# Two weight sums on GpSimd, a gate of one matmul, the first patches in one queue, and other tiles for the last image

## The chip, the cores and the metric

The kernel runs on one core of a Trainium2 chip. The metric is the device time of one execution in microseconds. Before the change the median of three runs is 2782.4 us (2776.88 to 2785.29). The profile is a further execution, with its own time.

## What is computed

The input is x, 16 images of 256 channels, 28x28, float32. The layer adds to x a block applied to its group norm:

```python
v = gn(x)                                            # 32 groups
h = relu(bn1(amm_conv3x3(v, centroids1, wsub1)))
h = bn2(amm_conv3x3(h, centroids2, wsub2))
s = sigmoid(relu(mean_hw(h) @ w1 + b1) @ w2 + b2)    # 256 -> 16 -> 256
out = x + relu(h * s[:, :, None, None] + v)
```

`amm_conv3x3` takes, for each channel and pixel, the nine values of the 3x3 patch, a softmax over 16 centroids by negative squared distance, the mean of the centroids under it (nine values again), and a product of these 256 x 9 values with `wsub`, a 2304 x 256 matrix.

## The kernel before

The work is a list of jobs. `at(cluster, sub, f, ...)` puts each under a key, and at the end (L1038) the keys are sorted and the jobs written out, so the order of each engine's instructions is the order of the keys. A layer of one image is eight clusters (`g = 8 * n`), for four blocks of (half of the channels, half of the pixels); each block takes two clusters of input, and its later steps lie in the clusters of the blocks behind it.

A block's steps: `patches` (L337) copies the shifted rows of the padded image ("home" in DRAM) into one of two tiles `pt`, in six transfers: three of 16 partitions by 8 (L342, always on SP's queue) and three of 8 by 8 (L346, on SP's queue, or on GpSimd's where `single` says so). `logits` (L351) are 32 small matmuls (64 records) in each cluster, `exps` (L365) their exponentials on ScalarE into tiles `e` of a pool with six buffers. `num_b` (L411) and `num_a` (L398) are the sums under the exponentials. VectorE inverts the denominators (L443) and spreads them over partitions (L458); the quotients q, tiles `qp` and `qo`, are made on GpSimd (L466) or VectorE (L477).

The product with wsub, a matrix of two by two parts, is done with seven products instead of eight. `mix` (L490) subtracts quotients of two blocks on GpSimd (five instructions for a pair of blocks: one at L492, four at L494). `combine` (L183) makes the summed weights S1, S2, S3, S4 of the first layer on VectorE; S2 = S1 - A11 and S4 = A12 - S2. `product` (L481) is nine matmuls into a PSUM bank, and `acc_copy` and `acc_add` (L515, L519) bring banks into the regions of the output; the eight banks are one ring. `PRODUCTS` says which weights a cluster's product reads: cluster 8 S3, 9 S2, 10 S4.

For the gate `se_hidden` (L751) multiplies the channel sums with w1 (four matmuls; w1, w2 and b1 padded to 128 columns or rows) and `se_gate` (L766) the hidden vector with w2 (two matmuls, one for each half of the channels). The weights are loaded by `load_se` (L202) in cluster 92, one of the tiles being that of `nhalf`. The images but the last have their closing passes spread over later clusters (`finish_gate`, `finish_norm`, `finish_sum`, `finish_relu`, `finish_add`); the last image uses `finish_norm` and `finish_fast` (L786, L805). `finish_norm` writes the group norm of x into the tile `xn` of tag "pb", of which there is one buffer. `flags` (L823), which checks the range of the denominators, uses the same tag for its tile `ok`.

Of the kernel before, what the change touches and what calls it, by code (L numbers as in the profile page):

```python
# [8 lines left out]
F32 = mybir.dt.float32  # L9
I32 = mybir.dt.int32  # L10
U32 = mybir.dt.uint32
AF = mybir.ActivationFunctionType
ALU = mybir.AluOpType
# [4 lines left out]
P = 128  # L18
# [5 lines left out]
N = RT * W  # L24
# [12 lines left out]
NPT = 2  # L37
# [30 lines left out]
def kernel(  # L68
# [20 lines left out]
    nc = tc.nc  # L89
    B, C, _ = x.shape  # L90
    NB = C // P
    RED = se_w1.shape[1]

    const = ctx.enter_context(tc.tile_pool(name="const", bufs=1))
    dram = ctx.enter_context(tc.tile_pool(name="dram", bufs=1, space=DRAM))
    small = ctx.enter_context(tc.tile_pool(name="small", bufs=2))
# [6 lines left out]
    def bank(name):  # L103
        return p_ring.tile([P, 512], F32, tag="ps", name=name)
# [21 lines left out]
    io = ctx.enter_context(tc.tile_pool(name="io", bufs=1))  # L126
    wpool = ctx.enter_context(tc.tile_pool(name="wpool", bufs=1))
    epool = ctx.enter_context(tc.tile_pool(name="epool", bufs=6))
# [54 lines left out]
    def combine(n):  # L183
        a, b, op = {
            "S1": ("S3", "A22", ALU.add), "S2": ("S1", "A11", ALU.subtract),
            "S4": ("A12", "S2", ALU.subtract), "S3": ("A11", "S3", ALU.subtract),
        }[n]
        nc.vector.tensor_tensor(wl[n], wl[a], wl[b], op)

    nhalf_sb = load(nhalf, "nhalf_sb")  # L190
    load_wd(None, 0)
# [3 lines left out]
    load_wd(None, 1)  # L195
    load_cw(0, 1)
    vecs = load(vec, "vecs", nc.gpsimd)
    w1_sb = [nhalf_sb, const.tile([P, P], F32, name="w1_sb")]
    w2_sb = const.tile([P, C], F32, name="w2_sb")
    b1_sb = const.tile([P, 1], F32, name="b1_sb")  # L200

    def load_se():  # L202
        for t in (*w1_sb, w2_sb, b1_sb):
            nc.gpsimd.memset(t, 0.0)
        for k in range(NB):
            nc.sync.dma_start(w1_sb[k][:, :RED], se_w1[k * P : (k + 1) * P, :])
        nc.sync.dma_start(w2_sb[:RED], se_w2)
        nc.sync.dma_start(b1_sb[:RED], se_b1.rearrange("(p o) -> p o", o=1))


    m_lo, m_hi, zero = kst[:, 0:1], kst[:, 1:2], kst[:, 2:3]
    m_cw = kst[:, 3:7]
# [283 lines left out]
    ys = {}  # L496
# [252 lines left out]
    se = {}  # L749

    def se_hidden(b):  # L751
        ysum = ys[b, "sum"]
        ps = bank("sep")[:, :1]
        n = 0
        for k in range(NB):
            for i in range(2):
                nc.tensor.matmul(
                    ps, lhsT=w1_sb[k], rhs=ysum[:, k, i : i + 1],
                    start=(n == 0), stop=(n == 2 * NB - 1),
                )  # L760
                n += 1
        hid = small.tile([P, 1], F32, name="se_hid")
        nc.scalar.activation(hid, ps, AF.Relu, bias=b1_sb, scale=1.0 / HW)
        se[b] = hid

    def se_gate(b):  # L766
        hid = se[b]
        ps = bank("sep")[:, :NB]
        for k in range(NB):
            nc.tensor.matmul(  # L770
                ps[:, k : k + 1], lhsT=w2_sb[:, k * P : (k + 1) * P], rhs=hid, start=True, stop=True
            )
        gt = small.tile([P, NB], F32, name="se_gt")
        for k in range(NB):
            nc.scalar.activation(
                gt[:, k : k + 1], ps[:, k : k + 1], AF.Exp, bias=nb2_sb[:, k : k + 1], scale=-1.0
            )
        nc.vector.tensor_scalar_add(gt, gt, 1.0)  # L778
        nc.vector.reciprocal(gt, gt)  # L779
        se[b] = gt  # L780
# [4 lines left out]

    def finish_norm(b, k):  # L786
        if k == 0:
            ys[b, "t"] = io.tile([P, 1568], F32, tag="pb", name="xn")
        nc.scalar.activation(
            ys[b, "t"][:, HW * k : HW * k + HW], xs[b][:, k], AF.Identity,  # L790
            bias=nrm[:, b, 2, k : k + 1], scale=nrm[:, b, 1, k : k + 1],
        )
# [28 lines left out]
    fi = const.tile([1, 1], I32, name="fi")  # L821

    def flags():  # L823
        ok = io.tile([P, 1568], F32, tag="pb", name="ok")[:, : 16 * B].rearrange("p (a n) -> p a n", a=2)
        nc.vector.tensor_scalar(ok[:, 0], wsum, LIM, None, op0=ALU.is_le)
        nc.vector.tensor_scalar(ok[:, 1], wsum, 0.0, None, op0=ALU.is_ge)
        nc.vector.tensor_reduce(fl[:, 0:1], ok.rearrange("p a n -> p (a n)"), axis=AX.X, op=ALU.min)
        nc.vector.tensor_scalar(fl[:, 0:1], fl[:, 0:1], -1.0, 1.0, op0=ALU.mult, op1=ALU.add)
        nc.vector.tensor_reduce(fl[:, 2:3], csum, axis=AX.X, op=ALU.max)
        nc.vector.tensor_scalar(fl[:, 2:3], fl[:, 2:3], CLIM, None, op0=ALU.is_gt)  # L830
        nc.vector.tensor_add(fl[:, 0:1], fl[:, 0:1], fl[:, 2:3])
        nc.vector.memset(fl[:, 3:4], 1.0)
# [8 lines left out]
    def at(cl, sub, f, *a, **kw):  # L841
        jobs.setdefault((cl, sub), []).append((f, a, kw))
# [20 lines left out]
    for j, u in enumerate(blocks):  # L863
        g = 2 * j
        u["w"] = j
        wide = u["l"] == 1 and u["hh"] == 0
        for p in range(2):
            u["pt", p] = pts[p]
            at(g + p - NPT, 0.5, patches, u, p, nc.gpsimd if g + p < 5 else None)
            for q in range(2):  # L870
                mm = 2 * p + q
                at(g + p, 0.1 + 0.1 * q, logits, u, mm)
                if wide and mm == 0:
                    at(g, 0.12, wide_copy, u, mm)
                    at(g, 0.9, wide_turn, u, mm)
                    at(g, 0.95, wide_sub, u, mm)
                    at(g + 1, 0.3, wide_back, u, mm)
                    at(g + 1, 0.9, wide_exp, u, mm)
                else:
                    at(g + p, 0.12 + 0.1 * q, exps, u, mm)  # L880
        at(g + 2, 1.3, num_b, u)
        at(g + 2, 1.4, split_b, u)
        at(g + 2, 1.5, join_b, u)
        at(g + 2, 1.6, recip_dve, u)
        at(g + 2, 1.7, spread, u, 4)
        at(g + 2, 1.71, scale_q, u, 4)
        for mm in range(2):
            at(g + 2, 1.35, num_a, u, mm)
            at(g + 2, 1.45, copy_a, u, mm)
            at(g + 3, 1.8, spread, u, mm)  # L890
            at(g + 3, 1.8, scale_q, u, mm)
        for mm in range(2, 4):
            at(*((g + 2, 1.8) if mm == 2 else (g + 3, 0.05)), spread, u, mm)
            at(g + 3, 1.0, num_a, u, mm)
            at(g + 3, 1.1, scale_a, u, mm)

    for l in range(2):
        for b in range(B):
# [26 lines left out]
            if l == 0:  # L925
                for o in range(2):
                    if b == 0:
                        at(g + 12 + o, 0.35, rank_score, o)
                        at(g + 12 + o, 0.6, rank_keep, o)
                        at(g + 12 + 2 * o, 0.65, h0_keep, o)  # L930
                    else:
                        for r in range(2):
                            at(g + 12 + o + (o and r), (0.5, 2.9)[r] if o == 0 else (2.4, 2.9)[r], to_home2, b, o, r)
                if b + 1 < B:
                    at(*((g - 1, 2.6) if b else (2, 1.65)), load_x, b + 1)
                    for q in range(NB):
                        at(g + (1 + q if b else 4), 0.3, gn_stats, b + 1, q)
                    at(g + (3 if b else 4), 2.1, gn_mean, b + 1)
                    at(g + 4, 2.1 if b else 2.2, gn_var, b + 1)
                    for q in range(NB):  # L940
                        at(g + 5, 0.9 if b else 0.3, gn_apply, b + 1, q)
                        at(g + 5, 1.9 if b or q else 0.9, to_home1, b + 1, q)
            else:
                last = b == B - 1
                at(*((g + 11, 0.6) if last else (g + 13, 2.6)), load_x, b, last)
                at(g + 13, 2.1, se_hidden, b)
                at(g + 14, 1.05 if last else 2.1, se_gate, b)
                for q in range(NB):
                    at(g + (13 if last else 19), 0.9, finish_norm, b, q)
                    if not last:  # L950
                        at(g + 19, 0.91, finish_gate, b, q)
                        at(g + 20, 0.05, finish_sum, b, q)
                        at(g + 20, 0.9, finish_relu, b, q)
                        at(g + 21, 0.05, finish_add, b, q)
                        at(g + 21, 0.06, store, b, q)
                    else:
                        at(g + 14, 1.92, finish_fast, b, q)
                        at(g + 14, 1.92, store, b, q)
                if b == B - 1:
                    at(g + 11, 0.95, flags)  # L960
                    at(g + 12, 2.9, flag_sum)

    at(1, 1.65, load_w, 0, "A11")
    at(3, 1.65, load_w, 0, "S3")
    at(3, 1.65, load_w, 0, "A22")
    at(6, 0.6, load_w, 0, "A12")
    for c, m in ((5, "S1"), (7, "S2"), (8, "S4"), (6, "S3")):
        at(c, 1.96, combine, m)
    for hh in range(2):
        at(6, 2.7, keep_wd, hh)  # L970
    for o in range(2):
# [223 lines left out]
```

## Time and profile before

| | |
|---|---|
| median of the runs | 2782.4 us |
| profiled execution | 2758.4 us |
| its span | 2756.9 us |
| instructions | 88069 |
| mean granted TensorE clock | 0.988 |
| MATMUL L485, w_S and w_A with qp | 708.3 and 521.2 us busy |
| MATMUL L356 (logits) | 535.2 us busy |
| MATMUL L403 and L417 | 409.0 and 371.2 us busy |
| POOL L494 (mixes) | 938.6 us busy, 1863 ns each |

In the profile, a row of a group says: line, engine, operation, what it writes and reads with shapes, count, busy time. PE is TensorE's matmuls, PEld its weight loads, DVE VectorE, ACT ScalarE, POOL GpSimd, SP the engine that issues most transfers. In a timeline each row has its start and length in us from the start of the span, and in brackets the idle time of the engine ahead of it with what ended it. float32 matmuls appear as two records each. The last 17.8 us of the span lie behind the last product on PE, and the first 28.9 before the first logits.

### The profile page before, as it was taken

The page shows a single profiled execution, that of the slowest core. Times are in us where ns is not written, and L with a number is a line of the kernel's source. Part 1 is how long each engine was busy: PE and PEld are TensorE (multiplying, and loading weights), DVE is VectorE, ACT ScalarE, POOL GpSimd, SP SyncE. Part 2 cuts the span into 40 slices and gives each one's busy share as a digit, 9 for nine tenths or more (in the row PEclk, how much of TensorE's full clock was granted, in tenths as well). Part 3 has the DMA queues.
Part 4 walks back from the last instruction along what each step waited for, and adds up shares of the span by engine and source line. Part 5 has one row for each costly group of instructions (what it writes and reads, how often), then busy time and mean ns, then how long its engine had stood idle before and what let it go on. Part 6 is the DMA issues. An engine that isn't in the chain of part 4 may idle for free. (4 is left out here: it accounts for less than half of the span.)

```text
span 2756.9 us, 88069 instructions
## 1 busy us (share of the span) xinstructions
PE 2670.6 (97%) x37076; PEld 1312.1 (48%) x37076; DVE 1730.1 (63%) x3945; ACT 1454.2 (53%) x3277; POOL 2073.0 (75%) x1427
## 2 busy tenths in 40 slices
PE   5699999999999999999999999999999999999997
PEld 2344444444444444444444455444444444444444
DVE  4866555565655565655576766666766666766664
ACT  3344455545455445455445566656565656555653
POOL 4656877668877767866678787788887788877787
PEclk9899999999999999999999999999999999999998
DMA  8564677546677656666575455445455545555541
GB/s 194 135 131 115 181 196 198 154 110 158 158 189 188 155 125 156 161 165 152 120 182 121 102 120 123 116 103 114 114 120 122 116 105 111 116 118 122 117 106 47
DMA packets 223281, 374.51 MB, mean 136 GB/s; under 512 B 30424, under 2 KB 193592, under 8 KB 222880
## 3 DMA queue, kind: packets, MB, share of 16 engines
q1 hardware_dynamic: 215744, 334.53, 52.6%
q0 software_dynamic: 7136, 34.27, 3.6%
q8 instruction: 296, 4.85, 0.8%
q14 instruction: 105, 0.86, 0.1%
HBM read 288.91 MB, written 79.80 MB: 134 GB/s over the span
## 5 line engine op out<-in xcount | busy, mean ns | idle before, releaser
L368 ACT ACTIVATE e<-lg 128x392 f32<-128x392 f32 x1920 | 777.7, 527 | 814.6 <-PE lg L356 812.3
L494 POOL TENSOR_TENSOR qp<-qp,qp 128x784 f32<-128x784 f32 x512 | 938.6, 1863 | 22.9 <-DVE qp L477 22.9
L485 PE MATMUL acc<-qp,w_S 128*128 128x392 f32 x2048 | 708.3, 496 | 5.2 <-POOL qp L494 5.2
L466 POOL TENSOR_TENSOR qp<-qp,rb 128x784 f32<-128x784 f32 x256 | 470.7, 1861 | 204.4 <-DVE rb L458 204.4
L356 PE MATMUL lg<-pt,wd 32*32 32x392 f32 x16384 | 535.2, 503 | 43.9 <-DVE half_sum L522 18.7
L458 DVE STREAM_SHUFFLE rb<-r 128x392 f32<-128x392 f32 x1024 | 551.2, 603 | 0.0
L485 PEld LDWEIGHTS acc<-qp,w_S 128*128 128x128 f32 x2048 | 387.4, 191 | 306.0 <-issue 15.9
L485 PE MATMUL acc<-qp,w_A 128*128 128x392 f32 x1536 | 521.2, 492 | 0.0
L437 DVE SCALAR_TENSOR_TENSOR r<-nb,kst,r 128x392 f32<-128x392 f32 x128 | 79.8, 623 | 563.4 <-ACT r L428 547.3
L403 PE MATMUL na<-e,cwa 64*32 64x392 f32 x8192 | 409.0, 496 | 3.9 <-issue 3.9
L485 PEld LDWEIGHTS acc<-qp,w_A 128*128 128x128 f32 x1536 | 291.8, 190 | 213.8
L417 PE MATMUL nb<-e,cwb 64*32 64x392 f32 x8192 | 371.2, 496 | 0.0
L356 PEld LDWEIGHTS lg<-pt,wd 32*32 32x32 f32 x16384 | 232.0, 103 | 274.8 <-issue 171.4
L443 DVE RECIPROCAL r<-r 128x392 f32<-128x392 f32 x128 | 331.8, 2592 | 0.0
L466 POOL TENSOR_TENSOR qo<-qo,rb 128x392 f32<-128x392 f32 x128 | 131.1, 1024 | 259.2 <-DVE rb L454 259.1
L477 DVE TENSOR_TENSOR qp<-na,rb 128x392 f32<-128x392 f32 x512 | 252.3, 555 | 64.6 <-PE na L403 61.7
L403 PEld LDWEIGHTS na<-e,cwa 64*32 64x32 f32 x8192 | 146.4, 106 | 230.2 <-ACT e L368 125.0
L417 PEld LDWEIGHTS nb<-e,cwb 64*32 64x32 f32 x8192 | 143.2, 107 | 220.6 <-issue 138.3
L471 ACT COPY qp<-na 128x392 f32<-128x392 f32 x512 | 211.6, 513 | 3.9 <-PE na L403 3.9
L428 ACT ACTIVATE r<-nb,kst 128x392 f32<-128x392 f32 x128 | 87.6, 685 | 102.7 <-PE nb L417 100.1
L492 POOL TENSOR_TENSOR qo<-qo,qo 128x392 f32<-128x392 f32 x128 | 130.8, 1022 | 2.2
L374 ACT COPY e<-lg 128x392 f32<-128x392 f32 x128 | 52.9, 500 | 150.6 <-PE lg L356 150.6
(146 smaller groups left out, 1810.7 us busy)
## 6 DMA issues: line engine op xcount, KB each, us to landing
pt<-home SPq DMA_DIRECT2D x768, 209.0 KB
pt<-home SPq DMA_DIRECT2D x753, 104.5 KB
home<-xpad SPq DMA_DIRECT2D x31, 899.0 KB
xt<-in_x SPq DMA_DIRECT2D x30, 784.0 KB
out_dram<-y SPq DMA_DIRECT2D x32, 392.0 KB
w_S<-d_wS SPq DMA_DIRECT2D x4, 576.0 KB
st<-in_wsub SPq DMA_DIRECT2D x4, 512.0 KB
st<-d_wa SPq DMA_DIRECT2D x16, 128.0 KB
```

Of the source, the lines that this page charges most:

```text
L356: nc.tensor.matmul(bk[32 * c : 32 * c + 32, :N].rearrange("p (r w) -> p r w", w=W), lhsT=wts["wd", u["hh"]][32 * i : 32 * i + 32, mm, c, : ...
L368: nc.scalar.activation(eg[:, i, :], bk[:, :N], AF.Exp, scale=2.0)
L403: nc.tensor.matmul(bs[r][32 * i : 32 * i + 32, :N], lhsT=wts["cwa", u["hh"]][64 * r : 64 * r + 64, mm, i, :], rhs=es[64 * r : 64 * r + 64, ...
L417: nc.tensor.matmul(bs[r][32 * i : 32 * i + 32, :N], lhsT=wts["cwb", u["hh"]][64 * r : 64 * r + 64, mm, i, :], rhs=es[64 * r : 64 * r + 64, ...
L443: nc.vector.reciprocal(u["r"], u["r"])
L458: nc.vector.stream_shuffle(rb[:, r, :], u["r"], mask_of(2 * mm + r))
L466: nc.gpsimd.tensor_tensor(q, q, u.pop(("rb", mm)), ALU.mult)
L471: nc.scalar.copy(u["q", 2 * mm + r], bk[:, :N])
L477: nc.vector.tensor_mul(u["q", 2 * mm + r], bk[:, :N], rb[:, r, :])
L485: nc.tensor.matmul(accs[key][:, :N], lhsT=wl[w][:, k, :], rhs=us["q", k], start=first and n == 0, stop=last and n == len(ks) - 1,)
L492: nc.gpsimd.tensor_tensor(out_u["q", 8], in0["q", 8], in1["q", 8], ALU.subtract)
L494: nc.gpsimd.tensor_tensor(pair(out_u, mm), pair(in0, mm), pair(in1, mm), ALU.subtract)
```

## The change

`combine` issues S2 and S4 on GpSimd; S2's key goes from sub 1.96 to 2.65 of cluster 7, behind that cluster's mixes. The first patches (the key of g + p = 0) have all six transfers on SP's queue. w1 is stored twice side by side, 32 columns, so that the hidden vector lies twice in 32 partitions; a constant `halves` with ones in the upper 16 rows of column 0 and the lower 16 of column 1 multiplies it on ScalarE, and one matmul with both halves of w2 stacked in 32 rows gives both columns of the gate. `load_se` clears nothing and makes six transfers instead of four. In the last image `xn` and `ok` are tiles `e`; `finish_norm` goes from (g + 13, 0.9) to (g + 12, 0.4), ahead of the relus of the image before it in ScalarE's order, and `flags` from sub 0.95 to 0.65 of cluster g + 11.

```diff
-        nc.vector.tensor_tensor(wl[n], wl[a], wl[b], op)
+        (nc.gpsimd if n in ("S2", "S4") else nc.vector).tensor_tensor(wl[n], wl[a], wl[b], op)
...
-    w1_sb = [nhalf_sb, const.tile([P, P], F32, name="w1_sb")]
-    w2_sb = const.tile([P, C], F32, name="w2_sb")
-    b1_sb = const.tile([P, 1], F32, name="b1_sb")
+    w1_sb = const.tile([P, NB, 2 * RED], F32, name="w1_sb")
+    w2_sb = const.tile([2 * RED, P], F32, name="w2_sb")
+    b1_sb = const.tile([2 * RED, 1], F32, name="b1_sb")
+    halves = const.tile([2 * RED, NB], F32, name="halves")
+    nc.gpsimd.memset(halves, 0.0)
+    nc.gpsimd.memset(halves[:RED, 0:1], 1.0)
+    nc.gpsimd.tensor_scalar(halves[:, 1:2], halves[:, 0:1], -1.0, 1.0, op0=ALU.mult, op1=ALU.add)
 
     def load_se():
-        for t in (*w1_sb, w2_sb, b1_sb):
-            nc.gpsimd.memset(t, 0.0)
         for k in range(NB):
-            nc.sync.dma_start(w1_sb[k][:, :RED], se_w1[k * P : (k + 1) * P, :])
-        nc.sync.dma_start(w2_sb[:RED], se_w2)
-        nc.sync.dma_start(b1_sb[:RED], se_b1.rearrange("(p o) -> p o", o=1))
-
+            nc.sync.dma_start(w1_sb[:, :, k * RED : (k + 1) * RED], se_w1.rearrange("(b p) r -> p b r", p=P))
+            nc.sync.dma_start(w2_sb[k * RED : (k + 1) * RED], se_w2[:, k * P : (k + 1) * P])
+            nc.sync.dma_start(b1_sb[k * RED : (k + 1) * RED], se_b1.rearrange("(p o) -> p o", o=1))
...
-        ps = bank("sep")[:, :1]
+        ps = bank("sep")[: 2 * RED, :1]
...
-                    ps, lhsT=w1_sb[k], rhs=ysum[:, k, i : i + 1],
+                    ps, lhsT=w1_sb[:, k, :], rhs=ysum[:, k, i : i + 1],
...
-        hid = small.tile([P, 1], F32, name="se_hid")
+        hid = small.tile([2 * RED, 1], F32, name="se_hid")
         nc.scalar.activation(hid, ps, AF.Relu, bias=b1_sb, scale=1.0 / HW)
-        se[b] = hid
+        se[b] = small.tile([2 * RED, NB], F32, name="se_hh")
+        nc.scalar.activation(se[b], halves, AF.Copy, scale=hid)
 
     def se_gate(b):
-        hid = se[b]
         ps = bank("sep")[:, :NB]
-        for k in range(NB):
-            nc.tensor.matmul(
-                ps[:, k : k + 1], lhsT=w2_sb[:, k * P : (k + 1) * P], rhs=hid, start=True, stop=True
-            )
+        nc.tensor.matmul(ps, lhsT=w2_sb, rhs=se[b], start=True, stop=True)
...
-            ys[b, "t"] = io.tile([P, 1568], F32, tag="pb", name="xn")
+            if b == B - 1:
+                ys[b, "t"] = epool.tile([P, 4, N], F32, tag="e", name="xn").rearrange("p i n -> p (i n)")
+            else:
+                ys[b, "t"] = io.tile([P, 1568], F32, tag="pb", name="xn")
...
-        ok = io.tile([P, 1568], F32, tag="pb", name="ok")[:, : 16 * B].rearrange("p (a n) -> p a n", a=2)
+        ok = epool.tile([P, 4, N], F32, tag="e", name="ok").rearrange("p i n -> p (i n)")
+        ok = ok[:, : 16 * B].rearrange("p (a n) -> p a n", a=2)
...
-            at(g + p - NPT, 0.5, patches, u, p, nc.gpsimd if g + p < 5 else None)
+            at(g + p - NPT, 0.5, patches, u, p, nc.gpsimd if 0 < g + p < 5 else None)
...
-                    at(g + (13 if last else 19), 0.9, finish_norm, b, q)
+                    at(*((g + 12, 0.4) if last else (g + 19, 0.9)), finish_norm, b, q)
...
-                    at(g + 11, 0.95, flags)
+                    at(g + 11, 0.65, flags)
...
-    for c, m in ((5, "S1"), (7, "S2"), (8, "S4"), (6, "S3")):
-        at(c, 1.96, combine, m)
+    for c, sub, m in ((5, 1.96, "S1"), (6, 1.96, "S3"), (7, 2.65, "S2"), (8, 1.96, "S4")):
+        at(c, sub, combine, m)
```

## The prediction

> **What bounds the kernel now.** I read the page first, then who waits for whom on PE, then the stretches where PE stands.
>
> ```profile
> PE 2670.6 (97%) x37076; PEld 1312.1 (48%) x37076; DVE 1730.1 (63%) x3945; ACT 1454.2 (53%) x3277; POOL 2073.0 (75%) x1427
> ```
>
> PE is busy 97%: 86.3 us idle of 2756.9. From 1400 to 2700 the table by stretches gives PE 1300.00 of 1300, so there every microsecond of PE work removed is gained; elsewhere only a removed wait is. PE's waits, longest first:
>
> ```profile
> PE lg L356 <- DVE half_sum L522: 18.7, 1, 18.7
> PE lg L356 <- DMA home<-xpad: 10.6, 1, 10.6
> PE lg L356 <- DMA pt<-home: 9.6, 6, 2.3
> ```
>
> The first is one wait. The timeline there, engine by engine (start, length; xN joins N instructions):
>
> ```profile
> 93.21 20.26 DVE L188 TENSOR_TENSOR w_S<-w_S,w_A 128x1152 f32<-128x1152 f32 x1
> 113.40 0.55 DVE L522 TENSOR_TENSOR half_sum<-acc,half_sum 128x392 f32<-128x392 f32 x1
> ...
> 92.33 1.03 POOL L492 TENSOR_TENSOR qo<-qo,qo 128x392 f32<-128x392 f32 x1
> 93.31 3.65 POOL L494 TENSOR_TENSOR qp<-qp,qp 128x784 f32<-128x784 f32 x2
> 96.92 3.61 POOL L466 TENSOR_TENSOR qp<-qp,rb 128x784 f32<-128x784 f32 x2
> 100.51 3.61 POOL L494 TENSOR_TENSOR qp<-qp,qp 128x784 f32<-128x784 f32 x2
> 104.09 1.00 POOL L492 TENSOR_TENSOR qo<-qo,qo 128x392 f32<-128x392 f32 x1
> 105.06 7.20 POOL L494 TENSOR_TENSOR qp<-qp,qp 128x784 f32<-128x784 f32 x4
> ...
> 114.00 1.53 PE L356 MATMUL lg<-pt,wd 32*32 32x392 f32 x8 [18.67 <-DVE half_sum L522]
> 115.46 4.94 PE L417 MATMUL nb<-e,cwb 64*32 64x392 f32 x64
> ```
>
> The Vector sum for S2 takes 20.26 us where its twin S4, alone, takes 1.42 (126.54). It ends 1.2 us after POOL's run, which has no gap from 75.98 to 112.26. Behind it stands half_sum (L522), which frees the PSUM bank that PE's next logits want. PE comes back slow: the clock row says 0.50 from 100 to 119, and 64 matmuls of nb take 4.94 instead of 2.86. The stall costs 18.67 + (1.53 - 0.25) + (4.94 - 2.86) = 22.0 us.
>
> **The sums S2 and S4 on GpSimd.** Two DVE instructions go (20.26 and 1.42), so half_sum runs at 93.2 and PE goes on. POOL gets two of 128x1152. Size: 392 columns take 1.02 and 784 take 1.86 (L492, L494), so 2.145 ns a column, 1.86 + 368 x 2.145 ns = 2.65 us each.
> S2 now stands last in that POOL run, behind the mixes of cluster 7, all of whose inputs are older: it runs 112.26 to 114.9. PE's product 9 reads it. PE's pace without stalls, from the clusters after (137.41 to 154.01, lg to the second product, 16.6, of which about 0.4 is a slow lg), brings PE from 93.39 to product 9 at 109.6; product 8's last mix, at 104.1, is needed at 105. So a new wait, PE on POOL, 115.05 - 109.6 = 5.4 us; behind it on PE stand product 9 and all later clusters. On POOL, behind S2, stand a scaling, S4 (to 118.6) and the scalings of block 3 (to 122.3); product 10, the first reader of S4, comes after product 9 and a cluster, near 128. S4 is hidden, 2.65 us at most if not.
> Clock after the new wait: in the trace 2.3 us of idle before 54.83 was followed by 0.50 from 54.9 to 58.3, 2.3 us before 75.70 by none, 18.7 by 6 us of it. The Trainium skill (TensorE: Matmul & The Clock Gate, "What's actually happening") says one idle window of about 3.4 us halves the clock; by that rule 5.4 us costs at least one half-speed window, 1.7 us, by the row at 75.70 nothing, by that at 114 3.3. I take 2.5. **S2 and S4: 22.0 - 5.4 - 2.5 = 14 us, bounds 13 to 16.6, a little either way for the pace: 12 to 17.**
> A rule speaks against this part. The skill (SBUF: State Buffer, "Who interferes with whom") has a Vector operation with two SBUF inputs blocked by a GpSimd one that reads SBUF until that one instruction finishes. By it S2 on DVE waits at most 1.86 us, the stall of 18.7 would not exist, and the change would only add the 5.4. The rows of S1 (76.74, 2.32 us) and S3 (86.66, 1.77 us), both inside POOL's run, keep to it; S2's row does not. I take S2's own row, because PE's wait and slow clock agree with it, and keep the rule as a rival.
>
> **First patches in SP's queue.** PE's first logits start at 28.94. By the packet times SP's six patch transfers (issued 16.51 to 20.3) run 17.7 to 24.5, and POOL's six, issued from 20.29 behind the norm of block 1, from 23.2 to 29.5, beside home's second half. The DMA is full meanwhile:
>
> ```profile
> 17.00:21.00 4.00, 0.72 (x3) 0.55 (x3) 1.03 (x6) 0.67 (x1) 2.11 (x5) 1.00 0.88 205
> 21.00:25.00 4.00, 0.00 (x0) 0.00 (x0) 0.00 (x0) 0.37 (x1) 2.79 (x6) 1.00 1.08 196
> 25.00:29.00 4.00, 0.06 (x9) 0.10 (x14) 0.00 (x0) 0.00 (x0) 0.00 (x0) 1.00 1.03 336
> ```
>
> (columns as the page's engines, then clock, DMA share, GB/s; I read the last two.) So only the order changes. Tile 0's 576 packets are now first: at some 125 a microsecond (767 packets in 6.8 us is 113 with the edges) 4.6 us, 17.7 to 22.4, PE at 22.8: 6.1 earlier. Then PE needs 6.6 us to the logits of tile 1 (28.94 to 35.50), at 29.4, when all transfers but the debt are through. The next block's patches are issued at 26.2 but meet the rest of home until 28.5, against 33.4 before: 4.9 earlier. From 40 the DMA is full again, and issues follow PE, so the shift stays. SP's three more issues (0.6 each) push tile 1's three by 1.8 and home's second half by 0.8 (21.4 to 22.2); its reader is issued at 42.9. POOL's queue loses three issues. **5 us, bounds 2 to 6.**
>
> **Gate and hidden layer.** In 15 images PE is the bound. Product end to the next logits is 0.79 us with the eight records of hidden (2520.89 to 2521.68) and 0.34 with the four of the gate (2529.91 to 2530.25). The gate's records halve: 0.17. The hidden weights go from 128 columns to 32; no row shows that with one column moving. The nearest: loading 32 columns (L356) 103 ns against 191, so 0.79 x 0.46 = 0.36; it could be 0, or 0.5. 15 x 0.53 = **8 us, bounds 2.5 to 10.** The new ACT copy (0.24 each, as L763) lies beside PE work; ACT is at 53%.
>
> **Weights of the gate.** Four POOL memsets (0.8 us) go, and with them SP's 8.9 us wait for them; two more SP issues at 0.4 to 0.6 come ahead of patches. PE has 60.00 of 60 from 1000 to 1060: 0, or -1 if that cover failed. The three small POOL operations at the start (0.4) lie ahead of gmat and the clearing of xpad, which ends at 5.04, 0.7 before PE's first need: 0.
>
> **Last image.** The end now, on DVE, ACT and PE:
>
> ```profile
> 2738.13 0.23 DVE L825 TENSOR_SCALAR ok<-wsum 128x128 f32<-128x128 f32 x1 [10.22 <-POOL y L795]
> 2740.82 1.59 ACT L800 ACTIVATE y<-y 128x784 f32<-128x784 f32 x2
> 2742.31 0.70 ACT L540 ACTIVATE y<-y,bnsh,bnsc 128x392 f32<-128x392 f32 x1
> 2743.01 1.96 ACT L789 ACTIVATE xn<-e,nrm 128x784 f32<-128x784 f32 x2
> 2743.15 1.01 PE L757 MATMUL sep<-ysum,w_sb 128*128 128x1 f32 x4 [1.32 <-ACT y L540]
> ```
>
> The flags wait for a shared tile, hold back region (0,0)'s sum, and so ACT's two relus come late and stand ahead of the last normalisation; xn stands ahead of se_hid. With other tiles the flags run near 2728, region (0,0) is summed at 2733.3 (product 11 ends 2733.2), xn runs 2734.8 to 2736.8, the relus after POOL's L795 to 2738.9. Late next is PE: product 12 ends 2739.10, flag sum and cast to 2739.5, last sum to 2740.05, normalisation to 2740.9; PE at 2740.95 instead of 2743.15, 2.2. Then se_hid no longer waits for xn (0.7), the gate is two records of 0.25 fewer (0.5), the new copy costs 0.3. **3 us.** Lower bound: the flags' two 128-wide instructions and one two-input sum run beside POOL's mixes, as L569 did (0.98 us against 0.23 for the like L576). Three waits for one POOL instruction bring them to 2733.4: nothing. Blocked like S2 until 2738.1, region (0,0) is late as before and xn now stands ahead of the relus: -1.5.
>
> **Sum.** 14 + 5 + 8 + 3 = 30 us. The profiled execution took 2758.4 (span 2756.9 and 1.5 around it): 2728. The median of the runs is 2782.4, 24 above it; a 1% change carries over: **2752 us**.
>
> **Rivals.**
> A, as summed: 2752, 0.68.
> B, the first shift is eaten by the full DMA after 40 and the flags are blocked: 14 + 1 + 8 - 1.5 = 21.5, 2761. For it: PE waits for patches at 54.83 and 75.70. Against: those issues follow PE. 0.17.
> C, the 20 us block is this execution's alone (S1 and S3 kept to one instruction). Then S2's move only costs 5.4 + 2.5: 16 - 8 = 8 gained, 2774. Against: POOL's run had no gap to miss, and the three runs lie within 0.3%. 0.10.
> D, slower: who gets the port is drawn anew by phase, and the block falls on another Vector operation in POOL's longer run (S1, S3, or the code spread at L569 and L572), with before's usual run having none. At the full 22 us: 16 - 8 - 22 = -14, 2796. It decides from 8 us of block. Against: POOL soon needs Vector results there (rb for L466 at 90.1), which cuts a block short. 0.05.
>
> A measurement of this kernel tells about 0.3% (8 us) from no change: faster A and B, 0.86 with a part of C; same 0.09; slower 0.05. Range: lower ends 12 + 2 + 2.5 - 1.5 = 15, upper 17 + 6 + 10 + 3.5 = 36.5, so 2767 to 2746, and 4 us for the spread of the runs shown: 2742 to 2770; C and D stay out.
>
> **What would show it.** DVE has no instruction near 20 us; PE's wait for half_sum is gone and one of about 5 us for POOL's w_S stands in its place, near 105 to 110; first logits near 23; product to logits 0.3 to 0.5 us shorter per image with sep; last hidden matmuls about 1.9 us after the last product. Wrong if an L188 of over 3 us remains, if the first logits start after 27, or if the distances around sep stay.

## The result and the profile after

The median of four runs of the changed kernel is 2751.9 us (2747.97 to 2756.05), beside 2782.6 (2776.88 to 2785.29) for the kernel before: a ratio of 0.9893, 95% interval 0.987 to 0.9915. Compared a second time, later and on another chip, it was 0.9925 (0.9902 to 0.9947). The forecast was 2752, in a range of 2742 to 2770.

The two first profiles do not show that difference: the profiled execution after took 2756.05 us, that of before 2758.4, which is 24 below before's median. So no total below is taken from two traces; totals come from the timed runs, and the traces are read for single waits and instructions.

After, the engines and the waits of PE, as the page and the list of who waits for whom have them:

```profile
PE 2684.1 (97%) x37044; PEld 1298.7 (47%) x37044; DVE 1717.0 (62%) x3943; ACT 1461.7 (53%) x3293; POOL 2076.5 (75%) x1425
```

```profile
PE lg L357 <- DMA pt<-home: 15.0, 6, 8.1
...
PE acc L486 <- POOL w_S L188: 3.1, 1, 3.1
```

The wait of 18.7 us for half_sum is gone, and one for GpSimd's S2 has come in its place. (Lines after L189 are one higher than before, and two from about L820.) The stretch that the forecast spoke of most, by engine, in the timeline of after:

```profile
117.68 6.74 DVE L570 TENSOR_SCALAR c<-c 128x144 f32<-128x144 f32 x1
126.55 1.03 DVE L523 TENSOR_TENSOR hpad<-acc,hpad 128x392 f32<-128x392 f32 x2
...
93.23 1.25 POOL L279 DMA_DIRECT2D d_wd<-wd  x2
114.58 2.61 POOL L188 TENSOR_TENSOR w_S<-w_S,w_A 128x1152 f32<-128x1152 f32 x1
118.13 2.60 POOL L188 TENSOR_TENSOR w_S<-w_A,w_S 128x1152 f32<-128x1152 f32 x1
120.70 3.63 POOL L467 TENSOR_TENSOR qp<-qp,rb 128x784 f32<-128x784 f32 x2
127.18 2.00 POOL L530 TENSOR_TENSOR hpad<-hpad,half_sum 128x392 f32<-128x392 f32 x2 [2.85 <-DVE hpad L523]
...
117.25 1.25 PE L486 MATMUL acc<-qo,w_S 128*128 128x392 f32 x2 [3.07 <-POOL w_S L188]
118.29 6.84 PE L486 MATMUL acc<-qp,w_S 128*128 128x392 f32 x16
```

S2 and S4 take 2.61 and 2.60 us on GpSimd, as worked out (2.65). Product 9 starts at 117.25 instead of 131.29, but runs slower than before, where its rows were:

```profile
131.29 0.93 PE L485 MATMUL acc<-qo,w_S 128*128 128x392 f32 x2
132.05 5.43 PE L485 MATMUL acc<-qp,w_S 128*128 128x392 f32 x16
```

The sums have left Vector, but a long instruction is there still: L570, which took 0.98 us before, takes 6.74 and ends at 124.42, just as GpSimd's run ends (120.70 + 3.63 = 124.33). What this means is the matter of the experiments; the two DMA issues (L279) in the first POOL row turn out to be the key.

The head and the tail, each with PE's rows:

```profile
26.41 3.35 PE L357 MATMUL lg<-pt,wd 32*32 32x392 f32 x64 [8.09 <-DMA pt<-home]
...
39.83 1.62 PE L357 MATMUL lg<-pt,wd 32*32 32x392 f32 x32 [3.69 <-DMA pt<-home]
```

The first logits come at 26.41 (before 28.94, forecast 22.8); the third at 39.83, where before had them at 40.14.

```profile
2735.11 5.43 PE L486 MATMUL acc<-qp,w_A 128*128 128x392 f32 x16
...
2742.21 0.28 PE L758 MATMUL sep<-ysum,w_sb 128*32 128x1 f32 x4 [1.42 <-ACT y L541]
```

The last hidden matmuls begin 1.67 us after the last product's end (2740.54).

### The profile page after: what moved, and what is told of

It is laid out like the page before. It is cut to its first block, busy times and chain, and to the rows that moved or that the text cites. A ratio compares the mean times of both kernels' runs of the same rounds, so it can differ in the third digit from the quotient of the medians.

```text
span 2754.6 us, 87978 instructions
## 1 busy us (share of the span) xinstructions
PE 2684.1 (97%) x37044; PEld 1298.7 (47%) x37044; DVE 1717.0 (62%) x3943; ACT 1461.7 (53%) x3293; POOL 2076.5 (75%) x1425
## 4 chain that ended last, share of the span: by engine, by line
PE 89%; DMA 3%; POOL 3%; SPq 1%; issue 1%; DVE 1%; ACT 1%; ACTq 0%; POOLq 0%; DVEq 0%
PE acc L486 47%; PE lg L357 17%; PE na L404 12%; PE nb L418 12%; DMA pt<-home 2%; POOL qp L495 2%; DMA home<-xpad 1%; SPq L343 1%; POOL qp L467 1%; SPq L347 1%; DMA row<-in_before 0%; ACT e L369 0%; POOL qo L493 0%; PE sep L758 0%; PE sep L770 0%
## 5 line engine op out<-in xcount | busy, mean ns | idle before, releaser
L357 PE MATMUL lg<-pt,wd 32*32 32x392 f32 x16384 | 555.9, 503 | 19.7 <-DMA pt<-home 15.0
L418 PE MATMUL nb<-e,cwb 64*32 64x392 f32 x8192 | 374.9, 499 | 2.6 <-issue 2.1
L444 DVE RECIPROCAL r<-r 128x392 f32<-128x392 f32 x128 | 331.8, 2592 | 0.0
L418 PEld LDWEIGHTS nb<-e,cwb 64*32 64x32 f32 x8192 | 143.8, 108 | 225.3 <-issue 140.8
```

The source lines that it names most:

```text
L357: nc.tensor.matmul(bk[32 * c : 32 * c + 32, :N].rearrange("p (r w) -> p r w", w=W), lhsT=wts["wd", u["hh"]][32 * i : 32 * i + 32, mm, c, : ...
L418: nc.tensor.matmul(bs[r][32 * i : 32 * i + 32, :N], lhsT=wts["cwb", u["hh"]][64 * r : 64 * r + 64, mm, i, :], rhs=es[64 * r : 64 * r + 64, ...
L444: nc.vector.reciprocal(u["r"], u["r"])
```

## The experiments

Three sets, each timed against the kernel before on one chip. The medians of before were 2765.1 us (29 runs) beside the first set, 2766.1 (23) beside the second, 2779.3 (15) beside the third. Where I write "the block" I mean a Vector instruction that takes many microseconds while GpSimd goes from one instruction to the next.

### The parts, one by one

**before_again** is the kernel before, unchanged, as a measure of what a comparison can tell.

> The kernel before, unchanged, traced again beside the others. Theory A (the 20 us block of the Vector sum S2 comes in every execution, and the first trace of before was an execution 24 us faster than its timed runs for another reason): same time, 0; S2's row again near 20 us, and the logits groups of the first layer about 20 us longer in total than in the first trace of before, as they are in the trace after. Rival C (the block was that execution's alone): no row of L188 over 3 us. Rival E (the first layer's slower logits come from the change): logits groups as short as in the first trace of before, span near 2757.

Measured: ratio 1.0014 (1.0003 to 1.0024). S2 took 20.24 us again. The block is therefore not of one execution. But of the 29 runs of before one took 2747.15 us, and the others 2755 and more. The interval leaves out 1 though the kernel is the same one, so a difference of some 0.2% (6 us) between two sets of runs is not read below as an effect unless a trace shows it too.

**sums** is before with the first part of the change alone:

```diff
-        nc.vector.tensor_tensor(wl[n], wl[a], wl[b], op)
+        (nc.gpsimd if n in ("S2", "S4") else nc.vector).tensor_tensor(wl[n], wl[a], wl[b], op)
...
-    for c, m in ((5, "S1"), (7, "S2"), (8, "S4"), (6, "S3")):
-        at(c, 1.96, combine, m)
+    for c, sub, m in ((5, 1.96, "S1"), (6, 1.96, "S3"), (7, 2.65, "S2"), (8, 1.96, "S4")):
+        at(c, sub, combine, m)
```

> S2 and S4 on GpSimd alone, with the new keys. Theory A: 14 us faster (12 to 17), PE waits some 3 to 5 us for POOL's S2. Rival C: 3 to 8 us slower.

Measured: median 2751.0, ratio 0.9955 (0.994 to 0.9971), 12 us gained, with an interval of 8 to 17. PE's new wait:

```profile
PE acc L485 <- POOL w_S L188: 3.4, 1, 3.4
```

That is some 60% of what the whole change gained when it was timed again (0.75% of 2766, 20.7 us), and some 40% of what it gained at first.

**first_patches** is before with the third part alone:

```diff
-            at(g + p - NPT, 0.5, patches, u, p, nc.gpsimd if g + p < 5 else None)
+            at(g + p - NPT, 0.5, patches, u, p, nc.gpsimd if 0 < g + p < 5 else None)
```

> The first patches all on SP's queue, nothing else. The prediction: 5 us faster (2 to 6). Rival B, as the trace after suggests (first logits 2.5 us earlier, but block 0's reciprocal 1.2 us later): within 2 us of no change, the start given back in the full DMA by 60 us.

Measured: ratio 1.0006 (0.9996 to 1.0015): nothing. The first logits came at 26.58 instead of 29.63 in before_again, and the third at 39.77 instead of 40.97, waiting longer for their patches:

```profile
39.77 3.35 PE L356 MATMUL lg<-pt,wd 32*32 32x392 f32 x64 [5.64 <-DMA pt<-home]
```

In before_again this wait was 3.63. The gain of 3.05 at the first logits is down to 1.2 at the third.

**gate** is before with the one-matmul gate, the 32 hidden columns and `load_se` of the change alone:

```diff
-    w1_sb = [nhalf_sb, const.tile([P, P], F32, name="w1_sb")]
-    w2_sb = const.tile([P, C], F32, name="w2_sb")
+    w1_sb = const.tile([P, NB, 2 * RED], F32, name="w1_sb")
+    w2_sb = const.tile([2 * RED, P], F32, name="w2_sb")
...
-        for k in range(NB):
-            nc.tensor.matmul(
-                ps[:, k : k + 1], lhsT=w2_sb[:, k * P : (k + 1) * P], rhs=hid, start=True, stop=True
-            )
+        nc.tensor.matmul(ps, lhsT=w2_sb, rhs=se[b], start=True, stop=True)
```

> The gate's part alone: 32 hidden rows, one matmul for the gate, six loads and no clearing. Theory A: 8 us faster, from 15 images of 0.55 us; its last image 0.5 to 1 us. Rival: the new copy on ScalarE or the loads take it back, within 3 us of no change.

Measured: ratio 0.9991 (0.9971 to 1.0012). The twelve runs fall into two heaps: 2746.6, 2747.3 and 2750.4, and nine from 2759.6 to 2771.0. The profiled one is the 2750.4, and it has no block: S2 takes 2.08 us there. Whether the nine slower ones had it is not on record, as they were not traced. So this ratio can't weigh a part of a few microseconds. The trace can: from block 67 to block 127 (each has one reciprocal, L444, whose start I compare) it takes 1231.8 us, and 1236.8 in both traces of the kernel before, before and before_again. Elsewhere it takes 1231.5 to 1232.5 us where the gate's part is in (after, after_again, s2_ahead) and 1236.8 to 1237.3 where it is not (six more traces). These 5.0 us are 0.44 in each block with the hidden layer and 0.15 in each with the gate, 0.58 an image, of which the next block mostly gives 0.06 back, less three jumps of 0.8 to 1.8 in single blocks.

**last** is before with the new tiles and keys of the last image alone:

```diff
-        ok = io.tile([P, 1568], F32, tag="pb", name="ok")[:, : 16 * B].rearrange("p (a n) -> p a n", a=2)
+        ok = epool.tile([P, 4, N], F32, tag="e", name="ok").rearrange("p i n -> p (i n)")
+        ok = ok[:, : 16 * B].rearrange("p (a n) -> p a n", a=2)
...
-                    at(g + (13 if last else 19), 0.9, finish_norm, b, q)
+                    at(*((g + 12, 0.4) if last else (g + 19, 0.9)), finish_norm, b, q)
```

> The last image's part alone: xn and ok in tiles e, the two new keys. The prediction's mechanism without the narrower gate: the normalisation of the last region 2.2 us earlier and se_hid no longer behind xn, 0.7: 3 us faster (2 to 3.5), seen as the distance from the last product's end to the two instructions of se_gt on VectorE, 7.6 us before, 4.6 here. Rival (the flags held up by POOL's mixes until they end): 1.5 us slower.

Measured: ratio 0.9987 (0.9974 to 1.0), 3.6 us, which the timed runs alone would not tell from nothing. The trace does: from the end of the last product to the end of the span it is 14.1 us, in before_again 17.9; to the two instructions of se_gt on VectorE it is 3.7, in before_again 7.5. Its profiled run, too, has no block (S2 2.05 us).

### Where S2 is put, and what blocks it

**after_again** is the change, on the chip of this set.

> The changed kernel beside the parts. If the parts add up, the sums' 12, the first patches' 0, the gate's 5 to 8 and the last image's 3 make 20 to 23 us, less than the 30 of the first measurement. If 30 us is the change's own worth on any chip, 30.

Measured: median 2743.3, ratio 0.9925 (0.9902 to 0.9947). PE waited 3.4 us for S2. L570 took 7.04 us.

**s2_ahead** is the change with GpSimd's S2 ahead of the mixes of cluster 7, so that PE need not wait for it:

```diff
-    for c, sub, m in ((5, 1.96, "S1"), (6, 1.96, "S3"), (7, 2.65, "S2"), (8, 1.96, "S4")):
+    for c, sub, m in ((5, 1.96, "S1"), (6, 1.96, "S3"), (7, 2.55, "S2"), (8, 1.96, "S4")):
```

> The changed kernel with one number altered: S2 on GpSimd ahead of the five mixes of blocks 2 and 0 instead of behind them. Theory A: PE's wait for POOL's S2 (3.1 us, and the slow clock behind it) goes, the last mix comes as product 9 reads it; 3 to 6 us faster than the change, if the mixes do not take the wait over. Rival (POOL's run is what PE waits for, in any order): no change.

Measured: 0.9937 (0.9914 to 0.996), no better than the change. The wait for S2 is gone, product 9 starts at 114.49, and another wait stands behind it:

```profile
122.94 0.84 PE L418 MATMUL nb<-e,cwb 64*32 64x392 f32 x2
128.35 3.51 PE L418 MATMUL nb<-e,cwb 64*32 64x392 f32 x38 [4.56 <-DVE hpad L523]
...
118.08 7.07 DVE L570 TENSOR_SCALAR c<-c 128x144 f32<-128x144 f32 x1
127.26 1.03 DVE L523 TENSOR_TENSOR hpad<-acc,hpad 128x392 f32<-128x392 f32 x2
```

L570 is blocked for 7.07 us, hpad (which frees a PSUM bank) stands behind it on Vector, and PE waits for hpad. In the change PE, held up by S2 until 117.25 and slow behind it, comes to these matmuls (L418) only at 127.39, when hpad (126.55 to 127.58) is all but done, so L570's block costs it nothing more; here it is bare.

**s2_late** is before with two small Vector reductions ahead of S2, to move its request to another moment of GpSimd's instruction:

```diff
+        if n == "S2":
+            late = const.tile([P, 2], F32, name="late")
+            for i in range(2):
+                nc.vector.tensor_reduce(late[:, i : i + 1], nhalf_sb, axis=AX.X, op=ALU.max)
```

> The kernel before, S2 still on VectorE, with two reductions of 128x128 (about 0.28 us each, results unused) ahead of it, so that its request for the port comes in the middle of a POOL instruction and not in the last 0.1 us of one. Theory P (a request at the boundary loses to every following POOL instruction, one in the middle gets the port at the next boundary): S2 takes 2 to 3.5 us, no block, 15 us faster than before. Rival (the unbroken POOL run blocks whatever the phase): 20 us again, no change. The reductions alone cost nothing on PE.

Measured: 0.9995 (0.998 to 1.0009), S2 19.85 us. Where in GpSimd's instruction the request falls does not decide.

What does came out of laying the traces side by side. In all with the block, GpSimd's two DMA issues of `keep_wd` (L278) end 0.9 to 1.3 us ahead of S2's request and GpSimd doesn't pause between. In the two without it, GpSimd did pause. This is GpSimd in gate:

```profile
89.11 1.25 POOL L279 DMA_DIRECT2D d_wd<-wd  x2
90.37 1.03 POOL L493 TENSOR_TENSOR qo<-qo,qo 128x392 f32<-128x392 f32 x1
92.43 3.68 POOL L495 TENSOR_TENSOR qp<-qp,qp 128x784 f32<-128x784 f32 x2 [1.03 <-DVE qp L478]
```

The bracket is a pause of 1.03 us between the issues and S2's request at 95.25. The pause is there because PE had waited 3.72 us for patches at 76 (2.30 in before), so Vector's quotients came later and GpSimd ran into a wait for them. So a theory, Q in the expectations: after a DMA issue of its own, GpSimd keeps Vector from the SBUF port that the two share until it next stops. Theory R, its rival: a run of GpSimd without a gap does so, whatever is in it.

### The issues taken away, replaced, moved

**keep_sync** is before with these two issues on SP's queue:

```diff
-        nc.gpsimd.dma_start(d_wd[0][:, 512 * hh : 512 * hh + 512], wts["wd", hh].rearrange("p a b c -> p (a b c)"))
+        nc.sync.dma_start(d_wd[0][:, 512 * hh : 512 * hh + 512], wts["wd", hh].rearrange("p a b c -> p (a b c)"))
```

> The kernel before with the two writes of the prepared weights (d_wd, L278) issued from SP instead of from GpSimd; S2 stays on Vector. Theory Q: the block comes from the two DMA issues of GpSimd that end 0.9 us ahead of S2's request, and lasts until GpSimd's next pause; without them S2 takes 1.8 to 3.1 us like S1 and S3, PE's wait for half_sum goes, and the median is 14 to 18 us lower than before in nearly all executions. Theory R: it is GpSimd's run without a gap, whatever is in it: S2 takes some 18 us again (the run is 1.2 us shorter), and the time is within 3 us of before.

Measured: median 2762.5, ratio 0.9938 (0.9919 to 0.9957), 17 us. S2 stays on Vector and is short:

```profile
94.72 2.07 DVE L188 TENSOR_TENSOR w_S<-w_S,w_A 128x1152 f32<-128x1152 f32 x1
96.72 0.55 DVE L522 TENSOR_TENSOR half_sum<-acc,half_sum 128x392 f32<-128x392 f32 x1
```

**keep_sync_full** fills the place of the issues with small sums, so that GpSimd's run is no shorter:

```diff
+        w = wts["wd", hh].rearrange("p a b c -> p (a b c)")
+        for i in range(2):
+            nc.gpsimd.tensor_tensor(fill, w[:, :56], w[:, :56], ALU.add)
+        nc.sync.dma_start(d_wd[0][:, 512 * hh : 512 * hh + 512], w)
```

> As keep_sync, but in place of the two issues GpSimd does four small sums of 56 columns (some 0.3 us each, results unused), so that its run is as long and as gapless as before. Theory Q: S2 in 1.8 to 3.1 us, the median 14 to 18 us lower than before. Theory R: S2 near 20 us and the time within 3 us of before. If keep_sync is free of the block and this one isn't, it was the place in the run and not the kind of instruction.

Measured: 0.9941 (0.992 to 0.9962). The run of GpSimd from 78.80 on has no gap before S2 and none for 25 us behind it, and S2 takes 1.38 us:

```profile
93.89 1.34 POOL L282 TENSOR_TENSOR fill<-wd 128x56 f32<-128x56 f32 x4
95.19 1.02 POOL L497 TENSOR_TENSOR qo<-qo,qo 128x392 f32<-128x392 f32 x1
96.17 4.79 POOL L499 TENSOR_TENSOR qp<-qp,qp 128x784 f32<-128x784 f32 x2
...
96.04 1.38 DVE L188 TENSOR_TENSOR w_S<-w_S,w_A 128x1152 f32<-128x1152 f32 x1
```

Here Vector is let in at the next boundary of GpSimd's instructions, and it is a mix that waits (4.79 us for two, instead of 3.65). So it is the kind of instruction, not the length of the run: theory R falls. Nor is it the transfers themselves, which take place here too, from SP's queue.

**keep_early** leaves the issues on GpSimd, but ahead of the mixes of cluster 5:

```diff
-        at(6, 2.7, keep_wd, hh)
+        at(5, 2.45, keep_wd, hh)
```

> The kernel before with GpSimd's two DMA issues moved ahead of the mixes of cluster 5 (from 91 to near 81 us), so that S3 and not S2 is the first two-input sum of Vector behind them. Theory Q: S3 is now blocked until GpSimd stops to wait for rb, behind the mixes, 4.5 us or more instead of 1.5 to 2.8; S2 behind that pause takes 1.8 to 3.1 us; the median 10 to 18 us lower than before. Theory R: S3 1.5 to 2.8 us, S2 near 20 us as before, and the time within 3 us of before.

Measured: 0.9935 (0.9911 to 0.9959). The block has moved to S3, the first of Vector's two-input sums behind the issues; then S2 is free. GpSimd and Vector in that trace:

```profile
80.52 1.25 POOL L278 DMA_DIRECT2D d_wd<-wd  x2
81.78 1.03 POOL L492 TENSOR_TENSOR qo<-qo,qo 128x392 f32<-128x392 f32 x1
82.75 7.28 POOL L494 TENSOR_TENSOR qp<-qp,qp 128x784 f32<-128x784 f32 x4
89.99 2.14 POOL L466 TENSOR_TENSOR qo<-qo,rb 128x392 f32<-128x392 f32 x1
...
85.50 5.76 DVE L188 TENSOR_TENSOR w_S<-w_A,w_S 128x1152 f32<-128x1152 f32 x1
...
96.10 2.06 DVE L188 TENSOR_TENSOR w_S<-w_S,w_A 128x1152 f32<-128x1152 f32 x1
```

S3 asks at 85.50, is passed over at the ends of mixes at 86.4 and 88.2, and is let in at 90.0, between the mixes and a scaling (which takes 2.14 us instead of 1.03, as it waits in turn). No idle time of GpSimd shows there, so "until it stops" is not proved to the letter.

**sums_back_keep_sync** is the change with all four sums back on Vector at their old places and the two issues on SP: the diffs of gate, last, first_patches and keep_sync, without that of sums.

> The change without its first part (all four sums on Vector, at their old places), with the two weight writes issued from SP. Theory Q: no block, and no wait of PE for GpSimd's S2 (3.4 us in the change, and what follows it); with the gate and the last image it is 22 to 26 us below before and 2 to 6 us below the change. Theory R: blocked in most executions like before, gate and last image alone, 5 to 9 us below before and some 14 above the change.

Measured: median 2750.4, ratio 0.9896 (0.9869 to 0.9922). S2 took 2.05 us, L570 0.98, and no wait for w_S is left. It stands as far below before as the change did in its two comparisons (0.9893 and 0.9925). The two were not run side by side, so that it beats the change is not shown; that a change of one queue does the work of the two moved sums is.

## Why the prediction was right, and where it was not

**S2 and S4, 14 us (12 to 17): the size is right and its cause was not known.** The three terms were 22.0 of block, less 5.4 of new wait, less 2.5 of slow clock. The new wait was 3.1 to 3.4. The slow clock: product 9 took 1.25 + 6.84 us instead of 0.93 + 5.43, 1.7 more; so an idle of 3.07 us was enough. After's granted clock (the third column from the right) shows where:

```profile
115.00:120.00 5.00, 2.75 (x5) 1.60 (x6) 5.00 (x12) 0.00 (x0) 5.00 (x3) 0.77 0.76 147
120.00:125.00 5.00, 5.00 (x14) 2.54 (x12) 4.93 (x4) 0.00 (x0) 4.33 (x3) 0.89 0.02 4
```

The idle window of about 3.4 us that the Trainium skill gives ("TensorE: Matmul & The Clock Gate", "What's actually happening") is longer than that idle; the price is what I had estimated from it for one window, 1.7. That makes 22.0 - 3.1 - 1.7 = 17, and the runs gave 12 (8 to 17), or 14 by the medians (2765.1 - 2751.0). So 17 lies at the edge of the interval. One run in 29 of before at 2747 is too few to explain a difference of the medians, and what does was not found.

The rule that I weighed, the Trainium skill's "SBUF: State Buffer", "Who interferes with whom", has Vector blocked for one GpSimd instruction. I set it aside for S2 because of the row, and S2's row was right. But the rule held for every sum that had no DMA issue of GpSimd ahead of it (S1 and S3 of before, S2 in keep_sync, 2.07, and keep_sync_full, 1.38), and for S2 in gate and last, where GpSimd had paused behind the issues. The forecast took the run without a gap as the cause. It was needed, but not enough; keep_sync_full has it and no block.

**Rival C** (the block is of that execution alone): wrong, since S2 took 20 us in each of before, before_again, first_patches and s2_late. But the block does stay out in some executions: it did in the profiled ones of gate and last, which differ from before in nothing that these stretches compute.

**Rival D** (the block falls on another instruction of Vector): its mechanism came about, not its price. The change left the issues where they were, so the next Vector instruction behind them that needs the port was blocked: L570, 6.7 to 7.1 us in all four traces with the sums on GpSimd and the issues kept (sums, after, after_again, s2_ahead), and 0.4 to 1.0 in the others. It was cheap as the wait for S2 had already made PE late for what stood behind L570, and s2_ahead shows the price once that wait is gone: 4.56 us. The reason against D, that GpSimd soon needs Vector's results and stops, is what ended it at 7.

**First patches, 5 us (2 to 6): wrong.** Two steps failed. "Tile 0's 576 packets are now first" at 125 a microsecond was to bring the first logits at 22.8; they came at 26.4, so that 2.5 of the 6.1 us were gained. Tile 1's transfers, issued from 20.25 on, shared the DMA with tile 0's from then on; that this is what held them back was not tried. And "issues follow PE, so the shift stays" failed: even that shift was given back by the third logits. The stretches of four microseconds show why, three of after and then the last of them in before:

```profile
21.00:25.00 4.00, 0.00 (x0) 0.00 (x0) 0.00 (x0) 0.33 (x1) 1.11 (x2) 1.00 1.04 184
25.00:29.00 4.00, 2.59 (x64) 1.17 (x64) 0.00 (x0) 1.00 (x3) 0.00 (x0) 1.00 1.06 205
29.00:33.00 4.00, 3.06 (x29) 1.03 (x9) 0.76 (x2) 2.22 (x6) 2.78 (x6) 1.00 0.79 252
...
29.00:33.00 4.00, 4.00 (x66) 1.57 (x66) 0.00 (x0) 2.48 (x7) 0.41 (x1) 1.00 0.05 7
```

In the last two columns, DMA share and GB/s, 25 to 29 is as full as before, but with 205 GB/s instead of 336. My reading, which no run takes apart, is that the large packets of home's second half, which before passed here, were pushed back and meet the patches of the next block. Before had a hole of DMA from 29 to 33 (share 0.05); the change fills it (0.79). The order was changed, the amount was not. That is the "meets the rest of home" of rival B, 0 us instead of its 1.

**Gate, 8 us (2.5 to 10): 0.58 an image in the trace, against 0.53 forecast, but 5 in the sum.** The rows of the hidden layer's matmuls fell from a median of 250 to 170 ns, so the 0.36 taken for 32 columns instead of 128 is 0.44. What was missing is that some of it is lost again in three single blocks (0.8 to 1.8 each, the same three in gate and in after). In gate's trace PE has one wait for instructions in this stretch, of 0.9; what the other jumps are was not found. Weights of the gate: 0 forecast, and PE has no wait for them in after.

**Last image, 3 us (-1.5 to 3.5): 3.8 in the trace.** The flags' two comparisons and their sum took 1.35, 1.88 and 0.81 us beside GpSimd, three waits of one instruction each, and were done at 2734.2, before region (0,0)'s sum at 2734.66. No block like S2's, and no issue either: GpSimd's last DMA issue in that trace is at 1465.

**The sum.** The parts come to 12 + 0 + 5 + 3.6 = 21 us, and the second comparison gave 20.7 (0.75% of 2766). The first gave 30.7, which is what was forecast as 30. The intervals of the two ratios overlap, so the agreement of 2751.9 with 2752 is in part luck: patches and gate were taken 8 us too high, and nothing measured was found in their place. And one premise, that the profiled execution is a fair stand-in for the runs, was poor: before's was 24 us below its median. From block 12 to block 66, in the first layer, the other thirteen traces, of whatever kernel, are 3 to 21 us longer than it. That stays open.

## What to carry to other kernels

When an instruction of Vector takes ten times its usual time beside GpSimd, look not only at what GpSimd computes but at what it issued since it last stood still; a DMA issue moved to another queue may be cheaper than moving the work. A move that leaves the cause where it is hands the block to the next instruction: look who is next and what stands behind it. And where the DMA is full, an earlier transfer is a later other one: ask for the hole that it will fill.

## What the runs showed of the hardware

A DMA issue on GpSimd's queue was followed by blocks of Vector of 5.8 (S3), 6.7 to 7.1 (L570) and 19.8 to 20.3 us (S2), through 3 to 12 GpSimd instructions, although the two issues took 1.25 us together and had ended up to 23 us before (93.23 + 1.25 to 117.68 in after). That is nine of the nine profiled runs in which such an instruction came before GpSimd's next pause. It struck a sum of two SBUF inputs and a TENSOR_SCALAR of one; spreads, reciprocals and sums with one input in PSUM ran on unharmed in the same stretch. That TENSOR_SCALAR is struck fits the Trainium skill ("SBUF: State Buffer", "Who interferes with whom"), which counts it among the operations that can take the port pair shared with GpSimd. Without the issue, or with a pause of 1 us behind it, the same instructions waited for one GpSimd instruction at most. In the block of after the DMA was all but idle (share 0.02 from 120 to 125, in the row shown above), so a transfer still under way is hardly what holds the port. GpSimd makes 91 issues in the trace of after and 94 in that of before, many with a run of 8 to 38 us without a pause behind them. In no such run but that of the two `keep_wd` issues is there a Vector instruction with two SBUF inputs, or a TENSOR_SCALAR. So the rest of these traces neither supports the rule nor speaks against it: it rests on this one pair of issues, moved and replaced. What in the hardware holds the port was not tried.
